# Second norm's low half by TensorE and ScalarE, logits from stacked weights, routing without its sum, and a new instruction order, in a one-core adaLN + SSM + MoE block

## The chip, the core and the metric

One core of one Trainium2 chip runs the whole kernel. The metric is the device time of one execution in microseconds. Below, PE is TensorE (PEld its weight loads), DVE is VectorE, ACT is ScalarE, POOL is GpSimd and SP is the engine that issues most DMAs.

## The reference

The input `x` is 8 sequences of 1024 rows of 256 channels. Everything is float32. Cut to what matters here:

```python
h = layernorm(x) * (1 + ca) + sa                  # ca, sa, ga, cb, sb, gb: per sequence, from c
x = x + ga * ssm(h)                               # scan over the rows, 16 states per channel:
                                                  #   state = exp(dt*A)*state + dt*u*B;  y = sum_n state*C
h = layernorm(x) * (1 + cb) + sb                  # the second norm
probs = softmax(h @ Wg)                           # 8 experts
top_vals, top_idx = top_k(probs, 2)
gates = top_vals / sum(top_vals)
x = x + gb * sum_over_the_two(gates * (h @ We[e] + be[e]))
```

## The kernel before

**Stages.** The rows are cut into 16 stages of 512 rows, two for each sequence. A stage is worked on channel-major: two halves `j` of 128 channels on the partitions, 512 rows along the free dimension. Stage `s` has three parts, and the parts of neighbouring stages overlap:

- `front(s)`: the first norm, its transposes into channels (`trans1`), modulation on ACT, the projection `proj` (L915), its copy `xd` (L920), the spill of B and C to DRAM and the broadcast loads `load B, C` (L1002, tile `bc`, a ring of 5 buffers), `dt` by softplus on ACT (L952) and `du` on POOL (L958).
- `state(s, n)` for n = 0 to 15: `v = du * B` on POOL (L1012, ring of 4), two `a = exp(dt*A)` on ACT (L1023, ring of 3), two scans on DVE (L1034), and the product with C, either on DVE (L1044, tile `hcD`, two instructions) or on POOL (L1049, tile `hs`, one instruction). `C_ENG` says which: in the middle 6 of 16 states go to POOL in a sequence's first stage and 7 in its second, in the last two stages 4. A `bc` buffer comes free when the product with C is done. PE adds the 16 products up in PSUM (L1097, tile `y`).
- `back(s)`: `x + y` on DVE, statistics, the second norm, its transposes (`trans2`, L852, tile `pt` in PSUM), the split of `h` into a rounded high part and a low part (below), the logits, the routing (L1225 to L1244, sixteen small steps, of which fifteen on DVE, and `gates` on DVE), and 16 expert pairs of six matmuls each (L1310: high x high, high x low weight, low x high weight). For all but the last stage ACT scales each pair by its gate (L1388, `wt`), PE adds the transposed results up (L1398, `ma`), ACT multiplies by gb (L1405), PE turns them back (L1413, `pf`) and a POOL DMA adds them to the output in DRAM. In the last stage, which is done in two parts of 256 rows, DVE adds the pairs up instead (L1333).

**The split.** PE runs these matmuls in a rounded float32 (fp32r). `hi` is ACT's modulation of `pt` written as fp32r; ACT then modulates `pt` again in place, exactly; DVE subtracts (L1169): `lo = pt - hi`. The PSUM tiles `pt`, `pe`, `pl`, `pf` and others share a ring of two banks, `psm`.

**The order.** Each instruction is recorded with a planned cost and a due time from the table `DUE`; a planner (`Plan.emit`) plays the engines through, always takes the ready instruction with the earliest due time, and so fixes one order for each engine, which is what the program holds. On the chip each engine works through its own list in order and waits where an operand or a buffer isn't ready.

Of the kernel before, what the change touches and what calls it, by code (L numbers as in the profile page):

```python
# [30 lines left out]
AHEAD = 1010.84  # L31
PATIENCE = {"ACT": 0.15, "DVE": 0.31, "PE": 0.32, "POOL": 0.26, "SP": 0}
# [5 lines left out]
    "-1/2": -610.4,  # L38
    "load c": -1959.77,
    "load wmod0": -1959.2,  # L40
    "load wmod1": -1903.73,
    "load wmod2": -1904.33,
    "load wmod3": -1902,
    "load W_x": -1905.67,
    "load W_dt": -1902.95,
    "load b_dt": -1896.67,
    "load A": -1896.69,
    "load D": -1905.33,
    "load Wg": 23.65,
    "Wg hi": 25.6,  # L50
    "Wg lo": -1879.07,
    "c^T": 19.14,
    "exp c": 576.64,
    "1 + exp c": -171.26,
    "1 / c": -583.34,
    "silu c": 49.75,
    "mod1": 597.1,
    "mod1 out": 214.25,
    "mod1 + 1": -23.47,
    "mod2": -1859.82,  # L60
    "mod2 out": -158.07,
    "mod3": 229.79,
    "mod3 out": -128.45,
    "mod3 + 1": -812.43,
    "ga0": -205.9,
    "ga1": -118.55,
    "ga2": -138.57,
    "ga3": -194.1,
    "gb0": 46.87,
    "gb1": 211.85,  # L70
    "gb2": -132.77,
    "gb3": -2055.94,
    "ga mod": -1469.96,
    "ga mod D": 75.2,
    "1 / ga": -434.12,
    "gb^T": -1935.95,
    "gb out": -1918.95,
    "gb store": -2004.44,
    "W_x^T": 597.29,
    "W_x out": -3.67,  # L80
    "W_dt^T": -1851.32,
    "W_dt out": -85.73,
    "exp A": -10.89,
    "-A": -388.67,
    "be rows": -3.96,
    "be hi": -24.41,
    "be lo": -124.92,
    "be": 74.87,
    "eps": -5318.24,
    "gates hi": (-1934.68, -2774.13, 20.33, -39.94, 880.55),  # L90
    "gates lo": (-26.36, -2354.31, -688.15, -51.05, -108.76),
    "load be": -1860.49,
    "iw": -610.42,
    "load x": (-1905.45, -1873.57, -1877.87, -1851.67, -345.66),
    "stats1": (224.71, 130.11, 139.36, -25.7, -59.05),
    "aggr1": (213.04, 114.8, -308.72, -24.67, 2.36),
    "before1": (-102.85, 91.85, 2.54, -14.87, -18.75),
    "rstd1": (-1104.41, -1916.02, -121.49, -268.12, -120.91),
    "shift1": (-507.66, -410.48, -1091.47, 527.46, 48.83),
    "norm1": (-144.62, -217.6, 35.93, 471.97, 36.59),  # L100
    "trans1_0": (-1936.2, -1160.43, -2075.71, -328.08, -365),
    "modg_0": (-1701.88, 396.46, -461.17, -6.71, -105.52),
    "modD_0": (-1695.18, -131.34, -462.04, -397.38, -105.23),
    "trans1_1": (-388.21, -18.09, -54.78, -626.82, -11.83),
    "modg_1": (-50.33, -1935.21, -197.83, -9.86, -10.79),
    "modD_1": (-11.21, -1916.99, -81.27, -9.63, -23.55),
    "W_x / ga": (66.75, 401.9, 25.85, -49.61, 434.89),
    "proj": (-596.85, -706.64, -714.41, -84.24, -74.21),
    "rows": (-2173.39, -2045.69, -3586.53, -10.82, -2052.7),
    "spill": (-4069.73, -5330.21, -46.16, -311.17, 432.09),  # L110
    "dt0": (-45.16, -658.43, -1891.19, -1934.24, -76.75),
    "softplus0": (-1126.61, -39.94, -137.57, -2844.14, -16.53),
    "dt1": (-2318.21, -2801.94, -207.93, -1934.26, -398.3),
    "softplus1": (-1126.2, -132.53, -379.84, -2844.16, -28.04),
    "du": (-195.14, -2811.82, -615.21, -365.67, -2224.29),
    "load B, C": (-5316.63, -1003.95, -1855.19, -4111.06, -3714.47),
    "v": (-12.17, -164.66, 175.11, 576.96, 952.78),
    "a0": (-22.27, -4.61, -6.54, -5.76, -3.99),
    "a1": (-22.41, -4.9, -6.15, -6.69, -4.35),
    "scan0": (-141.18, -335.17, -38.46, -51.65, -37.62),  # L120
    "keep0": (-1141.13, -1001.73, -2670.6, -1274.64, -1043.43),
    "C0": (-158.99, -48.75, -78.37, -397.8, -49.3),
    "scan1": (254.21, -7.15, -37.67, -52.31, -38.52),
    "keep1": (-281.8, -71.4, -191.93, -1247.6, -175.93),
    "C1": (-927.57, -102.36, -383.08, -272.81, -85.21),
    "C": (-434.46, -982.76, -611.91, -346.76, -4070.99),
    "y D": (-45.12, -33.67, -1893.89, -3.99, 105.31),
    "y": (-692.43, -142.1, -4.58, -4.37, -52.76),
    "y C": (-691.09, -2044.02, -79.98, -1517.96, -52.81),
    "load We": -1855,  # L130
    "We hi": -9.52,
    "We lo": -13.87,
    "x + y": (-1479.33, -1886.74, -1168.73, -231.3, 149.03),
    "store x": (-922.68, -81.4, -352.75, -1815.49, -3867.78),
    "stats2": (-1494.52, -143.82, -1171.26, -54.3, -45.3),
    "aggr2": (-211.14, -109.77, -383.59, -45.32, -9.65),
    "before2": (-6.93, 939.25, -95.98, -81.58, 4.88),
    "rstd2": (-1311.51, -927.35, -919.37, -30.48, -1009.27),
    "shift2": (-289.83, -684.01, -16.58, -27.32, -1671.91),
    "norm2": (-1.27, -217.09, 3.69, -457.58, 32.8),  # L140
    "trans2_0": (-119.41, -234.62, -25.53, -50.95, -76.58),
    "hi0": (-141.55, -203.81, -1226.77, -71.08, -264.52),
    "mod2_0": (-2325.4, 23.63, -1516.83, 17.71, 8.96),
    "lo0": (-954.37, -2006.41, -590.6, 934.22, -43.41),
    "trans2_1": (-68.72, -46.84, -1.98, -2278.83, -10.41),
    "hi1": (1.23, -85.95, -1275.97, -1245.79, 101.74),
    "mod2_1": (-321.5, -1489.76, -82.34, 2.7, -325.68),
    "lo1": (-1141.17, -296.15, -3856.65, 5.32, -1526.54),
    "logits^T": (-724.23, -896.69, -969.16, -194.29, -2895.23),
    "logits out": (-1885.54, -25.88, 4.38, -1907.25, -252.75),  # L150
    "logits": (-1228.11, -85.65, -1913.27, -106.24, -61.81),
    "route": (-1101.97, -1134.93, -1307.99, -656.85, -170.03),
    "gates": (-23.84, -155.06, -1508.55, -606.87, -165.13),
    "gates^T": (407.78, -236.26, -474.82, -43.28, -53.64),
    "gates out": (-77.16, -201.21, -201.01, -1117.77, 23.17),
    "biases": (-1847.78, -40.94, -21.25, 21.25, 22.67),
    "expert0": (-47.23, -150.46, 2.39, -24.85, 59.33),
    "weigh0": (-1667.95, -187.39, -1697.15, 581.79, -169.94),
    "sum0": (154.3, 300.84, -65.34, 25.8, 428.26),
    "gb": (-58.36, -0.34, -1235.11, 1080.88, -11.47),  # L160
    "turn": (45.89, -1931.1, -368.57, -9.4, 45.02),
    "out": (15.32, -128.7, -182.23, -5.57, 44.86),
    "expert1": (-18.1, -22.7, 0.47, 22.62, 93.37),
    "weigh1": (-2663.68, -186.81, -1239.07, -35.96, -23.31),
    "sum1": (49.93, -21.05, 3.3, -9.9, -95.83),
    "store": (96.93, -341.18, 142.45, -243.69, -21.12),
    "load gb": (-157.01, -157.01, -157.01, -157.01, -165.58),
    "last bias": -13.22,
    "last": 89.02,
    "last expert": -11.99,  # L170
    "last store": -219.81,
# [246 lines left out]
def kernel(  # L418
# [62 lines left out]
    wg_hi = cp.tile([P, DC, E], F32R, name="wg_hi")  # L481
    wg_lo = cp.tile([P, DC, E], F32R, name="wg_lo")
# [6 lines left out]
    eps = cp.tile([P, 1], F32, name="eps")  # L489
    gb_d = dram.tile([B, D], F32, name="gb_d", bufs=1)  # L490
# [18 lines left out]
    def setup():  # L509
# [20 lines left out]
        add("eps", "DVE", 0.01, lambda: nc.vector.memset(eps, EPS), w=[("eps",)])  # L530

# [35 lines left out]
        def wg():  # L567
# [6 lines left out]
        wgf = [w.rearrange("p k e -> p (k e)") for w in (wg_hi, wg_lo)]  # L574
        add("Wg hi", "ACT", 0.2, lambda: nc.scalar.copy(wgf[0], wg()), r=[wg_k], w=[("wg", 0)])
        add(
            "Wg lo", "DVE", 0.08,
            lambda: nc.vector.tensor_tensor(wgf[1], wg(), wgf[0].bitcast(F32), ALU.subtract),
# [267 lines left out]
    def to_channels(i, s, j, t, part):  # L846
        xn, pt, tg = ("xn", i, s, part), ("pt", i, s, part, j), part[1] - part[0]

        def f():
            p = psum(pt)  # L850
            for k in range(tg):
                nc.tensor.transpose(  # L852
                    p[:, k * P : (k + 1) * P], T[xn][:, k, j * P : (j + 1) * P], ident
                )

        plan.add(
            f"trans{i}_{j}", "PE", 0.11 * tg, t, f, r=[xn + (k,) for k in range(tg)], w=[pt],
            ring=[("psm", pt)] + [(k, (k, s, part)) for k in (("g", "gd") if i == 1 else ("hi", "lo"))],
        )
# [264 lines left out]
    def back(s, t, part):  # L1124
# [37 lines left out]
        def mod_hi(j):  # L1162
            modulate(new("hi", hi, [P, DC, CL], F32R)[:, j], 2, s, j, modT[:, 3:], part)
# [37 lines left out]
        def logits_out():  # L1201
            nc.scalar.copy(new("lg", lgt, [E, CL])[:, :cl], T[pl][:E, :cl])
# [322 lines left out]
```

## Time and profile before

| what | us |
|---|---|
| median of 3 runs (1077.4 to 1081.53) | 1079.51 |
| the profiled execution, by its run time | 1078.12 |
| its span, first to last instruction | 1076.2 |
| DVE busy in the span | 976.5 |
| PE busy | 948.7 |
| POOL busy | 928.3 |
| ACT busy | 840.0 |
| first scan starts (end of the lead-in) | 32.9 |
| stages 1 and 2 (from the first scan of one stage to that of the next) | 67.4 and 65.8 |
| stages 3 to 12 together | 611.4 |
| stages 13 to 15, to the end of the scans | 193.5 |
| from there to the end (the tail) | 46.8 |

"Busy" is the time in which an engine runs an instruction. The stages are cut at the first scan of each stage on DVE; each holds the back part of the stage before it. The average of stages 3 to 12 is 61.1 us.

### The profile page before, as it was taken

How to read it: one execution, taken by the hardware profiler on the slowest of the kernel's cores; microseconds unless marked ns; L12 is line 12 of the kernel's file. 1: busy time of each engine (PE TensorE's matmuls, PEld its weight loads, DVE VectorE, ACT ScalarE, POOL GpSimd, SP SyncE). 2: the span in 40 equal slices, each digit the busy share in tenths (PEclk: the TensorE clock that was granted, in tenths of full speed). 3: DMA queues.
4: the chain of work that ended last, by engine and by line, in shares of the span. 5: the costliest groups of instructions: out<-in, count | busy, mean ns of one | idle time of the engine just before them, and what ended most of it. 6: DMA issues, size and time to landing. Idle time of an engine off the chain costs nothing. (4 is left out here: it accounts for less than half of the span.)

```text
span 1076.2 us, 16579 instructions
## 1 busy us (share of the span) xinstructions
PE 948.7 (88%) x5525; PEld 746.9 (69%) x5525; DVE 976.5 (91%) x1506; ACT 840.0 (78%) x1835; POOL 928.3 (86%) x454
## 2 busy tenths in 40 slices
PE   6556897997989989898999999898998989899997
PEld 3444675775777858686776868677786767777765
DVE  4699897989999999999999999999999998989957
ACT  5755577887799877988799887988898788887651
POOL 3899776899999999899999999999999989888700
PEclk9666798998999989999999999999899999999999
DMA  6445333447545555454554653554555554365202
GB/s 208 143 176 176 137 139 112 144 165 192 173 162 160 176 159 177 131 185 157 153 202 120 208 164 138 169 179 157 151 195 143 175 155 159 119 178 153 102 1 44
DMA packets 67956, 165.13 MB, mean 153 GB/s; under 512 B 7056, under 2 KB 34080, under 8 KB 67872
## 3 DMA queue, kind: packets, MB, share of 16 engines
q1 hardware_dynamic: 59952, 156.23, 43.1%
q0 software_dynamic: 7920, 7.87, 5.3%
q8 instruction: 43, 0.70, 0.3%
q14 instruction: 41, 0.34, 0.1%
HBM read 146.76 MB, written 17.31 MB: 152 GB/s over the span
## 5 line engine op out<-in xcount | busy, mean ns | idle before, releaser
L1012 POOL TENSOR_TENSOR v<-du,bc 128x1024 f32<-128x1024 f32 x255 | 610.2, 2423 | 54.5 <-DMA bc<-bcd 35.7
L1023 ACT ACTIVATE a<-dt,negA 128x512 f32<-128x512 f32 x512 | 347.1, 692 | 54.8 <-DVE hcD L1044 45.0
L1049 POOL TENSOR_TENSOR hs<-hs,bc 128x1024 f32<-128x1024 f32 x96 | 232.3, 2419 | 16.2 <-ACT carry L1040 5.0
L1044 DVE TENSOR_TENSOR hcD<-a,bc 128x512 f32<-128x512 f32 x320 | 213.6, 682 | 15.1 <-ACT carry L1040 7.4
L1388 ACT ACTIVATE wt<-pe,G 128x256 f32<-128x256 f32 x480 | 200.8, 468 | 33.8 <-PE pe L1310 26.5
L1034 DVE TENSOR_TENSOR_SCAN a<-a,v 128x512 f32<-128x512 f32 x166 | 195.7, 1212 | 23.5 <-ACT a L1023 17.7
L1097 PE MATMUL y<-ident,hcD 128*128 128x128 f32 x1280 | 185.8, 286 | 30.9 <-DVE hcD L1044 30.7
L1034 DVE TENSOR_TENSOR_SCAN a<-a,carry,v 128x512 f32<-128x512 f32 x154 | 196.3, 1278 | 9.8 <-ACT a L1023 7.0
L1097 PEld LDWEIGHTS y<-ident,hcD 128*128 128x128 f32 x1280 | 154.8, 148 | 49.0 <-DVE hcD L1044 37.8
L1310 PE MATMUL pe<-we_hi,hi 128*128 128x512 f32 x512 | 181.7, 436 | 3.4 <-DVE lo L1169 1.1
L1310 PE MATMUL pe<-we_hi,lo 128*128 128x512 f32 x512 | 162.6, 399 | 0.0
L1310 PE MATMUL pe<-we_lo,hi 128*128 128x512 f32 x512 | 162.1, 398 | 0.0
L1398 PE MATMUL ma<-ident,wt 128*128 128x128 f32 x960 | 139.7, 274 | 0.6 <-ACT wt L1388 0.4
L1097 PE MATMUL y<-ident,hs 128*128 128x128 f32 x768 | 111.0, 290 | 24.0 <-POOL hs L1049 23.4
L1097 PEld LDWEIGHTS y<-ident,hs 128*128 128x128 f32 x768 | 92.0, 148 | 50.9 <-POOL hs L1049 40.5
L1398 PEld LDWEIGHTS ma<-ident,wt 128*128 128x128 f32 x960 | 112.5, 140 | 21.4 <-issue 4.6
L1034 DVE TENSOR_TENSOR_SCAN hs<-a,carry,v 128x512 f32<-128x512 f32 x102 | 126.0, 1268 | 1.3 <-ACT a L1023 1.3
L1310 PEld LDWEIGHTS pe<-we_lo,hi 128*128 128x128 f32 x512 | 97.1, 190 | 23.7
L1310 PEld LDWEIGHTS pe<-we_hi,lo 128*128 128x128 f32 x512 | 96.9, 189 | 23.7
L1034 DVE TENSOR_TENSOR_SCAN hs<-a,v 128x512 f32<-128x512 f32 x90 | 106.4, 1206 | 4.3 <-ACT a L1023 4.2
L1310 PEld LDWEIGHTS pe<-we_hi,hi 128*128 128x128 f32 x512 | 82.0, 192 | 16.6 <-ACT wt L1388 4.1
L822 ACT ACTIVATE xn<-x,ln 128x256 f32<-128x256 f32 x128 | 72.9, 598 | 1.6 <-POOL ln L814 1.6
(126 smaller groups left out, 969.2 us busy)
## 6 DMA issues: line engine op xcount, KB each, us to landing
bc<-bcd SPq DMA_DIRECT2D x256, 512.0 KB, 4.0
x<-in_L_attn_u_dram SPq DMA_DIRECT2D x16, 512.0 KB, 4.0
out_dram<-x SPq DMA_DIRECT2D x15, 512.0 KB, 3.0
out_dram<-of POOLq DMA_DIRECT2D x15, 512.0 KB, 9.1
wf<-in_L_ffn_We_dram SPq DMA_DIRECT2D x8, 256.0 KB, 4.0
wm<-in_L_wmod_dram SPq DMA_DIRECT2D x2, 512.0 KB
bcd<-xd SPq DMA_DIRECT2D x32, 32.0 KB, 3.7
wm<-in_L_wmod_dram SPq DMA_DIRECT2D x2, 256.0 KB, 6.0
```

The source lines that it names most:

```text
L822: nc.scalar.activation(new("xn", xn, [P, TG, D])[:, k, :], T[x][:, k0 + k, :], AF.Identity, bias=T[ln][:, 1, o + k : o + k + 1], scale=T[l ...
L1012: nc.gpsimd.tensor_tensor(new("v", v, [P, DC, CL])[:, :, :cl], T["du", s][:, :, :cl], both(T[bc][:, 0, :cl]), ALU.mult,)
L1023: nc.scalar.activation(new("a", a + (j,), [P, CL])[:, :cl], T["dt", s][:, j, :cl], AF.Exp, scale=negA[:, j, n : n + 1],)
L1034: nc.vector.tensor_tensor_scan(part(j), T[a + (j,)][:, :cl], T[v][:, j, :cl], init, ALU.mult, ALU.add)
L1044: nc.vector.tensor_tensor(new("hcD", hc, [P, DC, CL])[:, j, :cl], part(j), T[bc][:, 1, :cl], ALU.mult)
L1049: nc.gpsimd.tensor_tensor(o, o, both(T[bc][:, 1, :cl]), ALU.mult)
L1097: nc.tensor.matmul(new("y", y, [P, 2, D])[:, k % 2, j * P : (j + 1) * P], T[src][:, j, k * P : (k + 1) * P], ident, is_transpose=True, sta ...
L1310: nc.tensor.matmul(pe, T[v][:, j, k * P : (k + 1) * P], w[:, j, 2 * q : 2 * q + 2, :].rearrange("p e d -> p (e d)"), start=n == 0, stop=n ...
L1388: nc.scalar.activation(new("wt", wt, [P, 2, D])[:, i, :], T["pe", s, part, q, k][:, i * D : (i + 1) * D], AF.Copy, scale=T[G][:, k, e : e ...
L1398: nc.tensor.matmul(o[:, j, (k % 2) * P : (k % 2 + 1) * P], T["wt", s, q, k][:, i, j * P : (j + 1) * P], ident, is_transpose=True, start=Fa ...
```

## The change

- **Low part.** ACT first modulates `pt` in place, then copies it to `hi` in fp32r. A PE matmul with a constant minus identity (`less`) adds `-hi` to the PSUM bank that still holds `pt`, and ACT copies the difference out as `lo`. The DVE subtraction is gone. The transposes of `trans2` are written so that the accumulation stays open.
- **Logits.** The two parts of `Wg` lie side by side, 16 columns. `hi` is multiplied by all 16, `lo` by the first 8: four matmuls of 512 columns in place of six. The small transposes behind them become matmuls with a constant `fold` that adds the two halves.
- **Routing.** The sum of the two chosen weights is 1 + the second one, since the largest is exp(0). An ACT instruction, early in the routing, computes it; the reduction on DVE (L1239) is gone.
- **Order.** All due times, the look-ahead `AHEAD` and `PATIENCE` are new. In the planner an expert pair of stage `s` comes after the last expert of stage `s-1` of the half before it (`ex`) and after the turn-back of an earlier half (`td`).
- `C_ENG`, the rings and all else are as they were.

```diff
-AHEAD = 1010.84
-PATIENCE = {"ACT": 0.15, "DVE": 0.31, "PE": 0.32, "POOL": 0.26, "SP": 0}
+AHEAD = 1196.62
+PATIENCE = {"ACT": 0.15, "DVE": 0.4, "PE": 0.29, "POOL": 0.23, "SP": 0}
...
+        add("-I", "ACT", 0.25, lambda: nc.scalar.activation(negI, ident, AF.Copy, scale=-1.0), w=[("negI",)])
...
+        add("fold", "DVE", 0.07, lambda: nc.vector.reduce_sum(fold, ident[: 2 * E, : 2 * E].rearrange("p (i e) -> p e i", i=2), AX.X), w=[("wg", 2)])
...
                 nc.tensor.matmul(
+                    p[:, k * P : (k + 1) * P], T[xn][:, k, j * P : (j + 1) * P], ident,
+                    is_transpose=True, start=k == 0, stop=i == 1 and k == tg - 1, skip_group_check=True,
...
         def mod_hi(j):
-            modulate(new("hi", hi, [P, DC, CL], F32R)[:, j], 2, s, j, modT[:, 3:], part)
+            nc.scalar.copy(new("hi", hi, [P, DC, CL], F32R)[:, j, :cl], T["pt", 2, s, part, j][:, :cl])
...
+        def less(j):
+            nc.tensor.matmul(
+                T["pt", 2, s, part, j][:, :cl], negI, T[hi][:, j, :cl], start=False, stop=True,
+                skip_group_check=True,
+            )
         def low(j):
-            nc.vector.tensor_tensor(
-                new("lo", lo, [P, DC, CL], F32R)[:, j, :cl], T["pt", 2, s, part, j][:, :cl],
-                T[hi][:, j, :cl].bitcast(F32), ALU.subtract,
-            )
+            nc.scalar.copy(new("lo", lo, [P, DC, CL], F32R)[:, j, :cl], T["pt", 2, s, part, j][:, :cl])
...
-            for v, w in products:
+            for v, m in ((hi, 2 * E), (lo, E)):
                 for j in range(DC):
                     nc.tensor.matmul(
-                        lg[:E, :cl], (wg_hi, wg_lo)[w][:, j, :], T[v][:, j, :cl],
-                        start=n == 0, stop=n == 3 * DC - 1,
+                        lg[:m, :cl], wg_2[:, j, :m], T[v][:, j, :cl], start=n == 0, stop=n == 2 * DC - 1,
+                        skip_group_check=True,
...
-                nc.tensor.transpose(
-                    T[pl][:, k * E : (k + 1) * E], T[lgt][:, k * P : (k + 1) * P], ident[:E, :E]
+                nc.tensor.matmul(
+                    T[pl][:, k * E : (k + 1) * E], T[lgt][:, k * P : (k + 1) * P], fold, start=True, stop=True
...
-            lambda: red(col(3), view(1), AX.X, ALU.add),
-            lambda: nc.vector.reciprocal(col(3), col(3)),
+            nc.scalar.activation(col(3), col(1), AF.Identity, bias=1.0)
...
+            turns = [("ex", s - 1)] if s else []
+            if 2 * s + p > 2:
+                turns.append(("td", s - 2 + p, 1 - p))
...
-                        r=[hi, lo] + wes, w=[pe], ring=("psm", pe), duty=0.88, cold=1.76,
+                        r=[hi, lo] + wes + turns,
+                        w=[pe] + ([("ex", s)] if m == ends else []), ring=("psm", pe), duty=0.88, cold=1.76,
```

What the new due times make of the order, by reading both programs' instruction lists: expert pairs that stand before the last product with C of stages 1, 2 and 3 on PE are 13, 28 and 41 before and 9, 25 and 41 after, and from there on both have 16 for each stage until the end, where 237 of 240 become 236. The projection of stage 3 stands on PE behind 24 pairs before and behind 18 after; that of later stages, up to stage 13, behind the same number of pairs but behind 10 to 11 of the 16 sums of the stage in place of 8 to 10.

## The prediction

> **What bounds the kernel now.** I read the page's first part, then the time cut by stages, then the waits of the two busiest engines over the middle stages, then single shapes.
>
> ```profile
> PE 948.7 (88%) x5525; PEld 746.9 (69%) x5525; DVE 976.5 (91%) x1506; ACT 840.0 (78%) x1835; POOL 928.3 (86%) x454
> ```
>
> DVE looks like the bound, but 91% is an average over parts with different limits. Cut by stages (columns: stretch, length, then busy time and instructions of PE, PEld, DVE, ACT, POOL, then granted PE clock, DMA share, GB/s):
>
> ```profile
> 0.00:32.90 32.90, 23.05 (x82) 16.48 (x82) 10.89 (x58) 20.62 (x40) 16.27 (x21) 0.88 0.74 231
> 32.90:91.30 58.40, 30.86 (x127) 23.25 (x127) 54.28 (x61) 33.55 (x78) 52.97 (x25) 0.68 0.39 139
> 91.30:158.70 67.40, 56.65 (x289) 44.18 (x289) 61.37 (x90) 44.12 (x82) 53.49 (x26) 0.81 0.42 147
> 158.70:224.50 65.80, 57.15 (x337) 44.45 (x335) 57.03 (x89) 52.89 (x129) 53.65 (x27) 0.92 0.42 148
> 224.50:835.90 611.40, 563.34 (x3404) 446.46 (x3403) 584.48 (x870) 520.66 (x1138) 585.80 (x277) 0.98 0.53 165
> 835.90:1029.40 193.50, 179.11 (x1110) 144.22 (x1109) 179.45 (x255) 153.44 (x331) 162.52 (x77) 1.00 0.46 142
> 1029.40:1076.20 46.80, 38.49 (x186) 27.89 (x184) 28.97 (x86) 14.73 (x41) 3.57 (x7) 0.97 0.13 26
> ```
>
> In the ten middle stages DVE (584.5) and POOL (585.8 of 611.4, 96%) are equally full, and the change takes nothing from POOL. That is the main point: whatever DVE loses, POOL still needs 585.8. What it waits for there, and what DVE waits for:
>
> ```profile
> POOL v L1012 <- DMA bc<-bcd: 8.5, 9, 1.8
> POOL v L1012 <- DVE pl L1233: 2.8, 1, 2.8
> DVE a L1034 <- ACT a L1023: 4.4, 4, 1.7
> DVE a L1034 <- POOL v L1012: 3.5, 4, 1.2
> ```
>
> POOL's longest wait is for the B, C loads. A load can start only when the product with C of the state five earlier has freed its buffer. POOL's timeline shows the cycle:
>
> ```profile
> 499.59 2.35 POOL L1049 TENSOR_TENSOR hs<-hs,bc 128x1024 f32<-128x1024 f32 x1
> 501.91 2.35 POOL L1012 TENSOR_TENSOR v<-du,bc 128x1024 f32<-128x1024 f32 x1
> 504.48 0.25 POOL L1270 TENSOR_TENSOR gs<-G,gs 128x32 fp32r<-128x32 f32 x1 [0.22 <-ACT gs L1267]
> 506.10 4.70 POOL L1012 TENSOR_TENSOR v<-du,bc 128x1024 f32<-128x1024 f32 x2 [1.36 <-DMA bc<-bcd]
> ```
>
> The product ends at 501.9, and the `v` that needs the buffer starts at 506.1: about 4.1 us for release, load and landing. With only one `v` in between, POOL stands still for 1.4 to 1.8 us.
>
> **The change part by part.** The rows that price it:
>
> ```profile
> L1169 DVE TENSOR_TENSOR lo<-pt,hi 128x512 fp32r<-128x512 f32 x30 | 20.4, 680 | 1.4 <-ACT pt L863 1.2
> L1419 ACT COPY of<-pf 128x512 f32<-128x512 f32 x30 | 17.5, 584 | 6.1 <-PE pf L1413 6.0
> L863 ACT ACTIVATE hi<-pt,modT 128x512 fp32r<-128x512 f32 x30 | 23.3, 782 | 2.0 <-PE pt L852 2.0
> L1195 PE MATMUL pl<-hi,wg_lo 128*8 128x512 f32 x30 | 9.6, 404 | 0.0
> ```
>
> *DVE.* Gone are 30 x 0.680 + 4 x 0.422 (the last stage's 256 columns) = 22.1 us of L1169, and 17 reductions of 0.19 = 3.2. Per middle stage that is 2 x 0.680 + 0.19 = 1.55, 15.5 in the ten: DVE falls to 569, 93%.
>
> *ACT.* Two copies for `lo` are added, two modulations become copies, one small instruction (0.184, as L1227) comes in the routing. With the nearest copy out of PSUM, 0.584: 2 x 0.584 - 2 x (0.782 - 0.584) + 0.184 = +0.95 a stage. ACT is idle (611.4 - 520.7) / 10 = 9.1 a stage, so the load is free. Its waits are not (second rival). The Trainium skill speaks against this move: "ScalarE: Activation LUTs", section Rules for kernel authors, gives additions to VectorE and budgets about 0.3 us and 0.83 ns an element for ScalarE, by my estimate 0.725 for 512. The trace shows a copy at 0.584 against DVE's subtraction at 0.680. By the page ACT would gain 4 x 0.14 = 0.6 more a stage, still inside its idle time, and the sum would stay.
>
> *PE.* `less` is two matmuls of 512 columns a stage, 0.40 each by L1195's row; the logits lose two at 0.40. Nil. No row shows a matmul with 16 output columns; 8 and 128 both take 0.40, so I take no difference. The `fold` matmuls replace transposes one for one (0.21 each); between nothing and, at the 0.30 that other small transposes take, 0.4 us a stage, hidden in PE's (611.4 - 563.3) / 10 = 4.8 of idle time. Without that cover: +6 in all.
>
> *Lead-in (to 32.9).* Setup steps move on all queues, SP's loads too. The first scan now stands behind five small DVE steps of the second modulation. They cost some 4.5 us before, but stood between the first scans then. What is late next is the second scan, at 39.3 before; POOL's first `v` follows a softplus that is put behind four normalisations (2.1 us). I take 0, with -2 and +2 as bounds.
>
> *Stages 1 and 2* are 133.2 long where two middle stages take 122.3: 10.9 too many. Stage 2 is short of data for stage 3: PE worked 28 expert pairs in the first two stages, and the projection of stage 3 stood behind 24 of them; POOL then waited for the loads (13.2 us in the two stages, up to 5.4 at once). Now it is 25 pairs, and the projection stands behind 18, five states earlier. The three pairs fall into stage 3, where PE is idle for 7 us. The bounds are all 10.9 and nothing; I take half, -5.5. A rule speaks against it: "TensorE: Matmul & The Clock Gate", section Part 1, says that the array's clock stays halved until a window of about 3.4 us has been busy. The rows agree: 0.68 in stage 0, 0.81 in stage 1, 1.0 later. With 9 pairs in place of 13 in stage 1, PE is less busy and may stay slow. By that rule I would put 0 in place of -5.5.
>
> *Stages 3 to 12.* POOL is idle for 25.6. The part that the buffers force: in the order of before, a product and the `v` that reuses its buffer have one `v` between them in six places, and some 3.8 us in three; with 4.1 needed, that makes 10.8. In the new order it is nine places and five: 16.1. So the stages can't go below 585.8 + 16.1 = 601.9, a gain of at most 9.5; if the other 14.8 of waiting (on late scans, behind blocks of routing) stay whole, they lose 5.3. DVE's 1.55 a stage should remove part: I take half of the 14.8, and get -2.1.
>
> *Stages 13 to 15.* POOL has 31 us to spare, DVE and PE are level at 179 of 193.5. DVE loses 6 x 0.680 + 3 x 0.19 = 4.7, PE one expert pair (some 1.5). I take -3; bounds -4.7 and, for a 3.9 us stop of POOL that the new order makes in stage 14 (a product and its `v` with almost nothing between), +3.
>
> *Tail.* Behind the last sum PE now has 20 pairs to do instead of 19, but three fewer `ma` groups. The chain of the first part (transpose, modulate, `hi`, `less`, `lo`, logits) gets two hops between ACT and PE where DVE stood ready: +1.5. For the second part an expert pair (1.7 us) stands between `hi` and `less`, and PE then has seven pairs behind the second turn of the gates instead of six. I take +3, bounds 0 and +6.
>
> Sum: 0 - 5.5 - 2.1 - 3 + 3 = -7.6. The profiled execution took 1078.1 (its span 1076.2), so 1070.5; the median, 1.4 above it, would give 1071.9. I say 1071.
>
> **The rivals.**
>
> *No change (POOL keeps the time).* POOL is as full as DVE, the new order forces 5.3 more waiting, stages 1 and 2 lose by the slow clock what they gain in order, the tail takes 3: -2 to +5, 1077 to 1084. For it: the 96% row. Against it: POOL was not the limit in stages 1, 2 and 13 to 15.
>
> *Slower: `lo` waits on ACT for `less`.* In most middle stages an expert pair (six matmuls, 1.7 us) stands on PE right before one of the two `less`, and only 0.9 to 2.3 us of ACT work stands between `hi` and `lo`. ACT works in order: behind a late `lo` stand the `a` of the next scans, with a ring of three, and DVE waits for them. 30 halves at up to 1.5 us. It decides from 0.43 us for each half that reaches the scans: 13 us, which turns -7.6 into +5.4. At 0.75 the time is 1071 + 22 = 1093. Against it: DVE waits for `a` only 6.6 us in the ten stages now, and the planner put work there.
>
> *Larger gain (DVE was the pace).* All of DVE's 25.3 comes out, since POOL's waits were DVE's lateness: 1078 - 25 + 3 = 1056. Against it: the floor of 601.9.
>
> **How the numbers follow.** Forecast 0.54, with its own range of 1060 to 1074; larger gain 0.08; no change 0.20; slower 0.18. About 0.5% (5.4 us) is what a measurement of this kernel can tell from no change; faster means under 1074.1, slower over 1084.9. The range goes from 1056 to 1087: it leaves out half of the larger gain and two thirds of the slower case, some 0.17 together.
>
> **What would show it.** Right: DVE busy near 951, POOL still near 928, stages 1 and 2 near 127 together, the ten middle stages between 602 and 612 with POOL over 96% busy, the tail near 50. Wrong: long waits of DVE for L1036's `a`, of ACT's `lo` for PE, or a first scan after 35.

## The result, and the profile after

The changed kernel took 1088.83 us (median of four runs, 1086.65 to 1090.82), beside 1078.76 for before in the same runs: a ratio of 1.0075, 95% interval 1.0053 to 1.0098. It is slower, by 10 us in the medians and 8 by the ratio, where 1071 was forecast with a range to 1087. Its profiled execution took 1090.8 (span 1089.0), 12.8 more in span than the profiled one of before.

First the busy times of the page (engine, busy us, share of the span, instructions):

```profile
PE 965.8 (89%) x5589; PEld 766.8 (70%) x5589; DVE 952.4 (87%) x1456; ACT 855.6 (79%) x1887; POOL 927.7 (85%) x454
```

The work moved as worked out: DVE lost 24.1 us (22.1 + 3.2 forecast), ACT gained 15.6 (0.95 for each stage is 15.2), POOL kept its 928. Only PE is off: nil was said, with at most some 6 for `fold`; it gained 17.1. So the time was not lost to work on DVE, ACT or POOL. The stages show where it went (stretch, length, then busy us and instructions of PE, PEld, DVE, ACT, POOL, granted PE clock, DMA share, GB/s); the last cut is the end of the last scan, which lies at 1027.9 in before. The cut used there ahead of the prediction, 1029.4, is 1.5 us later; by the cut of this table its 193.5 and 46.8 become 192.0 and 48.3, and its last row becomes the one that stands below these, by itself:

```profile
0.00:32.40 32.40, 19.99 (x86) 14.31 (x86) 13.94 (x64) 20.07 (x40) 14.60 (x20) 0.96 0.73 224
32.40:86.50 54.10, 29.82 (x122) 22.26 (x123) 50.89 (x56) 34.03 (x79) 53.88 (x25) 0.66 0.45 157
86.50:152.50 66.00, 52.06 (x296) 41.32 (x296) 63.02 (x97) 44.81 (x84) 54.35 (x26) 0.91 0.45 150
152.50:212.60 60.10, 54.86 (x311) 43.45 (x310) 53.01 (x76) 52.36 (x128) 54.03 (x26) 0.89 0.45 151
212.60:838.50 625.90, 579.82 (x3467) 464.14 (x3465) 569.68 (x842) 532.42 (x1177) 585.13 (x277) 0.97 0.54 163
838.50:967.20 128.70, 121.65 (x723) 96.63 (x722) 114.32 (x164) 107.97 (x239) 118.39 (x56) 0.96 0.49 150
967.20:1032.70 65.50, 61.68 (x396) 51.15 (x395) 59.44 (x81) 46.44 (x97) 43.78 (x22) 1.00 0.40 121
1032.70:1089.00 56.30, 45.95 (x201) 33.48 (x199) 28.12 (x82) 17.45 (x50) 3.57 (x7) 0.90 0.11 21
```

```profile
1027.90:1076.20 48.30, 39.44 (x192) 28.64 (x191) 29.69 (x87) 15.16 (x42) 3.57 (x7) 0.97 0.12 25
```

| stretch | before | after | difference | forecast |
|---|---|---|---|---|
| lead-in | 32.9 | 32.4 | -0.5 | 0 |
| stage 0 | 58.4 | 54.1 | -4.3 | not in the sum |
| stages 1 and 2 | 133.2 | 126.1 | -7.1 | -5.5 |
| stages 3 to 12 | 611.4 | 625.9 | +14.5 | -2.1 (-9.5 to +5.3) |
| stages 13 to 15, to the last scan's end | 192.0 | 194.2 | +2.2 | -3 (-4.7 to +3) |
| tail | 48.3 | 56.3 | +8.0 | +3 (0 to +6) |

At the start of stage 3 the new kernel is 11.9 us ahead. It then loses 14.5 in the ten middle stages, where POOL's work is the same to 0.7 us and DVE has 14.8 less. Both stand still instead: DVE for 56.2 us (26.9 in before), POOL for 40.8 (25.6). What POOL and DVE wait for there (in all, times, longest):

```profile
POOL v L1025 <- DMA bc<-bcd: 19.6, 15, 3.5
POOL gs L1293 <- ACT gs L1290: 6.0, 4, 2.4
```

```profile
DVE a L1047 <- ACT a L1036: 16.4, 18, 1.9
DVE hcD L1057 <- ACT carry L1053: 11.0, 26, 1.4
DVE a L1047 <- POOL v L1025: 8.3, 10, 2.4
DVE hs L1047 <- ACT a L1036: 3.2, 7, 0.7
```

and, of before, the two rows of DVE that the prediction does not show:

```profile
DVE hcD L1044 <- ACT carry L1040: 2.2, 6, 0.7
DVE hs L1034 <- ACT a L1023: 2.2, 3, 1.4
```

POOL's wait for the loads has gone from 8.5 to 19.6. One of them in the timeline of POOL:

```profile
798.86 2.37 POOL L1062 TENSOR_TENSOR hs<-hs,bc 128x1024 f32<-128x1024 f32 x1
801.19 2.40 POOL L1025 TENSOR_TENSOR v<-du,bc 128x1024 f32<-128x1024 f32 x1
807.08 2.35 POOL L1025 TENSOR_TENSOR v<-du,bc 128x1024 f32<-128x1024 f32 x1 [3.50 <-DMA bc<-bcd]
```

The product with C ends at 801.2, one `v` follows, and the next `v` has to wait for the load into the buffer that the product freed. That takes 5.9 us here, where the prediction put 4.1.

Some of these waits are put down to another releaser, so I added them up another way: for each `v` whose buffer a product on POOL had held, the idle time right before it, if there was any. In the middle stages of before that is 12 times, 14.1 us in all, with 3.9 to 5.2 us from the product's end to the start of `v`; in after 16 times, 25.2 us, mostly 3.8 to 5.9, once 9.7 (there the load was issued late). In the others the load is issued within 0.03 us of the product's end, so the rest is the load itself. One of the waits that the profile puts down to PE:

```profile
568.82 2.38 POOL L1062 TENSOR_TENSOR hs<-hs,bc 128x1024 f32<-128x1024 f32 x1
...
571.99 2.90 POOL L1025 TENSOR_TENSOR v<-du,bc 128x1024 f32<-128x1024 f32 x1
576.62 2.35 POOL L1025 TENSOR_TENSOR v<-du,bc 128x1024 f32<-128x1024 f32 x1 [1.74 <-PE pv L959]
```

Here 5.4 us pass from the product's end (571.2) to the `v`.

### The profile page after: what moved, and what is told of

It is laid out like the page before. It is cut to its first block, busy times and chain, and to the rows that moved or that the text cites. A ratio compares the mean times of both kernels' runs of the same rounds, so it can differ in the third digit from the quotient of the medians.

```text
span 1089.0 us, 16751 instructions
## 1 busy us (share of the span) xinstructions
PE 965.8 (89%) x5589; PEld 766.8 (70%) x5589; DVE 952.4 (87%) x1456; ACT 855.6 (79%) x1887; POOL 927.7 (85%) x454
## 5 line engine op out<-in xcount | busy, mean ns | idle before, releaser
L1062 POOL TENSOR_TENSOR hs<-hs,bc 128x1024 f32<-128x1024 f32 x96 | 228.6, 2382 | 13.1 <-DVE hs L1047 6.3
L1047 DVE TENSOR_TENSOR_SCAN a<-a,v 128x512 f32<-128x512 f32 x166 | 197.3, 1217 | 26.4 <-ACT a L1036 14.1
L1333 PE MATMUL pe<-we_hi,hi 128*128 128x512 f32 x512 | 184.7, 442 | 2.7 <-ACT dt L965 1.4
L1421 PE MATMUL ma<-ident,wt 128*128 128x128 f32 x960 | 142.9, 275 | 0.8 <-ACT wt L1411 0.8
L1110 PE MATMUL y<-ident,hs 128*128 128x128 f32 x768 | 112.9, 294 | 31.2 <-POOL hs L1062 30.6
```

The lines of the kernel that those rows point to most:

```text
L1047: nc.vector.tensor_tensor_scan(part(j), T[a + (j,)][:, :cl], T[v][:, j, :cl], init, ALU.mult, ALU.add)
L1062: nc.gpsimd.tensor_tensor(o, o, both(T[bc][:, 1, :cl]), ALU.mult)
L1110: nc.tensor.matmul(new("y", y, [P, 2, D])[:, k % 2, j * P : (j + 1) * P], T[src][:, j, k * P : (k + 1) * P], ident, is_transpose=True, sta ...
L1333: nc.tensor.matmul(pe, T[v][:, j, k * P : (k + 1) * P], w[:, j, 2 * q : 2 * q + 2, :].rearrange("p e d -> p (e d)"), start=n == 0, stop=n ...
L1421: nc.tensor.matmul(o[:, j, (k % 2) * P : (k % 2 + 1) * P], T["wt", s, q, k][:, i, j * P : (j + 1) * P], ident, is_transpose=True, start=Fa ...
```

## Experiments

In all of them the planner is not run; its order is written out as a list, so that parts and order can be exchanged one by one:

```diff
-        while len(order) < len(ops):
...
-            best, soon = None, dma.next()
...
+        order = ORDER
```

"Parts" are the three changes of the code (low part, logits, routing), "order" is the sequence in which all queues get their instructions. "Spliced" is the order of after up to the first scan of stage 4, and the order of before from there:

```diff
-ORDER = before
+first = after[: after.index(("scan0", stage 4, state 0))]
+ORDER = first + [step for step in before if step not in first]
```

Where a part is taken alone, its hunks of the change are applied and the others are not; a step that only one version has stands beside the step that it follows (`less` behind its `hi`). The ratio is to before, in the same runs, with its 95% interval. Before itself took 1078.5 to 1081.1 in these groups of runs, so the ratios are what to compare.

| parts | order | buffers for B, C | us | ratio |
|---|---|---|---|---|
| before | before | 5 | 1078.8 | 1 |
| after | before | 5 | 1091.0 | 1.0120 (1.0100 to 1.0140) |
| before | after | 5 | 1093.4 | 1.0136 (1.0116 to 1.0156) |
| after | after | 5 | 1088.8 | 1.0075 (1.0053 to 1.0098) |
| before | spliced | 5 | 1070.7 | 0.9927 (0.9899 to 0.9956) |
| after | spliced | 5 | 1078.5 | 0.9998 (0.9975 to 1.0022) |
| low part alone | spliced | 5 | 1082.2 | 1.0014 (0.9991 to 1.0036) |
| logits alone | spliced | 5 | 1074.8 | 0.9955 (0.9927 to 0.9983) |
| routing alone | spliced | 5 | 1071.0 | 0.9916 (0.9888 to 0.9943) |
| before | before | 6 | 1071.2 | 0.9925 (0.9909 to 0.9941) |
| before | after | 6 | 1082.6 | 1.0036 (1.0010 to 1.0061) |
| after | after | 6 | 1070.6 | 0.9908 (0.9884 to 0.9932) |
| before | spliced | 6 | 1062.4 | 0.9844 (0.9824 to 0.9863) |
| low part alone | spliced | 6 | 1074.2 | 0.9943 (0.9924 to 0.9962) |
| after | spliced | 6 | 1070.3 | 0.9919 (0.9892 to 0.9946) |
| after | after, last stage as before | 6 | 1070.9 | 0.9921 (0.9890 to 0.9951) |

**Order or parts.** The first pair exchanges them.

> All parts of before (the low part by the subtraction on DVE, six logit matmuls, four transposes, the sum of the gates) on each queue in the order of after; a step that both have stands where after has it. Theory ORDER: the loss of after (middle ten stages 611.4 to 625.9, tail 48.3 to 56.3) is made by the new order of the queues, so it stays: 1085 to 1095, middle at least 620, tail 54 to 57. Theory PARTS: the loss is made by the new steps themselves (the low part waits for PE on ACT, PE has 17 us more work), and the order only brings the 11.9 us that stages 0 to 2 gained: 1066 to 1072, middle near 611.

> All parts of after in the order of before; the matmul with minus identity stands right behind its copy of the high part. ORDER: 1073 to 1081 (DVE has 25 us less and most of that hides behind POOL), middle 605 to 613, tail 48 to 51. PARTS: 1090 to 1100, since the middle loses its 14.5 us and the gain of stages 0 to 2, which is the order's, is missing; middle 622 or more, with DVE waiting for the decay factors of ACT.

Measured: 1093.4 and 1091.0. The old parts in the new order lose as ORDER said (middle 623.0, tail 54.6). But the new parts in the old order lose too, as PARTS said, though at other places: middle 615.5 (+4.1), stages 13 and 14 +3.3, lead-in +2.6 (before with six buffers, below, has +1.7 there with no other change, so part of this may be the execution), tail 50.0 (+1.7). Either one alone costs 1.2 to 1.4%, both together 0.75%: the two don't add. With the old parts the new order loses about as much in the middle and tail as after does, and it is the only order in which the new parts gain something (0.6%). That the sizes are alike doesn't make the cause the same; the sixth buffer, below, parts them.

**The start alone.**

> Parts of before; the order of after up to the first scan of stage 4 (273.2 us in after, 286.2 in before), the order of before from there. Both theories: 1078.8 - 13.0 = 1066, if the start of after is worth what its trace shows and is not given back behind the joint; 1072 or more if some of it is.

> Parts of after, the same splice. ORDER: 1060 to 1068, as the old parts in this splice or a little less. PARTS: 1066 + 14 = 1080.

Measured: 1070.7 and 1078.5. The start of the new order is worth 0.7% with nothing else changed, about 8 us; part of the expected 13 is given back behind the joint (stage 4 takes 65.0, 60.3 in before). The new parts cost 0.7% in this order; their trace has 1.1 us of that in the middle stages, 4.1 in stage 14 and 2.7 behind it.

**Which part.**

> The spliced order, with one of the three new parts: the low part by PE and ACT. With the old parts this order took 1070.7, with all three new ones 1078.5. Theory LOW (the 7.8 us belong to the low part: two more hops between ACT and PE, and the copies stand before the next decay factors on ACT): 1076 to 1079. Rival FOLD (they belong to the logits, whose last step takes 17.4 us of PE where it took 7.0): 1070 to 1072 here. Rival SPREAD (each part a third): 1073.

> The spliced order, with only the stacked logits. LOW: 1070 to 1072 (two matmuls of 0.40 go, and the eight small ones take 0.65 us a stage more: level). FOLD: 1075 to 1078. SPREAD: 1073.

> The spliced order, with only the routing without its sum: 3.2 us less on DVE, 3.0 more on ACT. LOW and FOLD: 1068 to 1071. SPREAD: 1073.

Measured: 1.0014, 0.9955 and 0.9916, beside 0.9927 with none. The low part costs 0.9%, all that the three cost together. The routing without its sum can't be told from nothing; the logits neither, since the intervals overlap, though a third of the cost (0.3%) can't be ruled out for them. LOW stands; FOLD and SPREAD don't, since each needs the low part alone to cost little or a third.

**The ring of the loads.** One more buffer takes away what makes POOL wait, and nothing else:

```diff
-    "dt": 2, "du": 2, "bc": 5, "v": 4, "hs": 3, "carry": 2, "hcD": 3,
+    "dt": 2, "du": 2, "bc": 6, "v": 4, "hs": 3, "carry": 2, "hcD": 3,
```

> After itself, with six buffers for the B, C loads in place of five, every queue in the same order. Theory RING: the middle stages of after are long because POOL waits for loads that wait for a product with C (19.6 us of waits in the ten stages, 8.5 before): those waits go, the middle falls from 625.9 to 612 or less, the time to 1074 or less. Rival A (DVE waits for ACT's decay factors, 19.6 us against 6.6, whatever POOL does): POOL's waits go to other releasers, and the time falls by less than 5, to 1084 or more.

Measured: 1070.55, ratio 0.9908: 18 us less. The ten middle stages of this run (611.4 in before), and what is left of POOL's wait for loads in them:

```profile
210.98:821.04 610.06, 572.50 (x3459) 461.87 (x3458) 568.35 (x842) 530.99 (x1173) 586.00 (x277) 0.97 0.55 167
```

```profile
POOL v L1210 <- DMA bc<-bcd: 0.9, 1, 0.9
```

and DVE's waits for ACT:

```profile
DVE a L1232 <- ACT a L1221: 11.3, 15, 1.8
DVE hcD L1242 <- ACT carry L1238: 6.3, 22, 0.4
...
DVE hs L1232 <- ACT a L1221: 3.1, 6, 0.7
```

The middle falls from 625.9 to 610.1 with every queue in the same order and the same work, and POOL's wait for loads from 19.6 to 0.9. RING is right for after, rival A is not: DVE's waits for ACT (`a` and carry together) fall along with POOL's, from 30.6 to 20.7 us.

> Before itself (its parts, its order) with six buffers for the B, C loads. In its ten middle stages the first drive that finds its buffer held by a product with C waits 12 times, 14.1 us in all (16 times, 25.2 us, in after). If those waits are time: 1078.8 - 14 = 1065, or 1068 if DVE (584.5 of 611.4) gives some of it back. Rival (DVE is as full as POOL, so its work keeps the time): 1074 to 1079.

> Before's parts in after's order, now with six buffers; with five it took 1.0136 of before. If the ring is what the new order loses by: 1078.8 x 1.0136 - 18 = 1075 or less, as much gained as after gained (1.0075 to 0.9908). If DVE, with 22 us of work more than in after, is late by itself: above 1082.

> Before's parts, after's order up to stage 4, before's order from there, six buffers. Gains of the splice (0.9927 of before) and of the ring (10 to 14 us) together: 1058 to 1062. If both gains are the same waits: 1066 to 1070.

Measured: 0.9925, 1.0036 and 0.9844. Before gains 8 us from the sixth buffer where after gains 18. With it, before and after are level (0.9925 and 0.9908). The old parts in the new order gain 11, less than after; they end at the 1082 that was named for a late DVE. In the new order, then, the new parts are worth 1.3% with six buffers; that this is the lighter DVE is argued, not shown by itself.

The traces say where the ring counts. In the middle stages the waits for a buffer held by POOL fall from 14.1 to 1.0 us in before, from 25.2 to 0.9 in after and from 21.8 to 1.6 with the old parts in the new order. But the stages get shorter by only 2.9 us (611.4 to 608.5), 15.8 and 3.2 (623.0 to 619.8). A counted wait is time only where nothing else would have made POOL wait. With the old parts in the new order something else does: DVE's waits for ACT's `a` and carry stay at 20.5 us with either ring, and POOL's `hs` waits 10.7 us for ACT's carry where it waited 1.3. So it is the new order together with the new parts that the ring held; what keeps the old parts long in that order stays open.

The old parts in the spliced order with six buffers are the fastest kernel of this study, 1062.4; the two gains add.

**How the low part costs.** Two runs repeat the spliced pair where the ring no longer holds POOL:

> Spliced order, old parts but for the low part by PE and ACT, six buffers. With five the low part cost 0.9927 to 1.0014, 9.4 us. If it costs by itself (DVE stands for decay factors that ACT computes behind the copies): 0.9844 to about 0.993, 1071. If it costs through the ring (later scans, later products, later loads): 0.9844 to 0.987, at most 1066.

> Spliced order, all new parts, six buffers. Low part by itself: 0.992, about 1070. Through the ring: at most 0.987, 1065.

Measured: 0.9943 and 0.9919, beside 0.9844 with the old parts. The cost stays at 1.0%, so it isn't the ring's. In the middle stages of the low part alone DVE has 9.5 us less work (573.6 for 583.1) and they are 8.0 longer (617.7 for 609.7); stages 14 and 15 and the tail add 4 more. What DVE waits for in the middle, old low part:

```profile
DVE a L1221 <- ACT a L1210: 5.2, 5, 1.7
DVE hcD L1231 <- ACT carry L1227: 4.6, 6, 2.7
```

and new low part:

```profile
DVE hcD L1237 <- ACT carry L1233: 11.6, 15, 2.9
DVE a L1227 <- ACT a L1216: 9.8, 14, 1.7
```

Between the starts of one state's scans and the next's, the new low part adds 0.9 us in state 7 of the even middle stages (6.87 for 5.96), 4.5 of the 8.0 us in the five of them, and at most 0.24 in their other states. In the odd ones state 7 loses 0.9 too, but states 5 and 6 win 0.7 back. In state 7 the second half is split. At the passage from state 6 to state 7, with the old low part (spliced, five buffers, stage 6) DVE does

```profile
426.99 2.32 DVE L1217 TENSOR_TENSOR_SCAN a<-a,v 128x512 f32<-128x512 f32 x2
429.21 1.27 DVE L1227 TENSOR_TENSOR hcD<-a,bc 128x512 f32<-128x512 f32 x2
430.40 0.68 DVE L1352 TENSOR_TENSOR lo<-pt,hi 128x512 fp32r<-128x512 f32 x1
431.00 2.33 DVE L1217 TENSOR_TENSOR_SCAN a<-a,v 128x512 f32<-128x512 f32 x2
433.24 0.67 DVE L1227 TENSOR_TENSOR hcD<-a,bc 128x512 f32<-128x512 f32 x1
```

and with the new one (same place and order):

```profile
425.67 2.61 DVE L1227 TENSOR_TENSOR_SCAN a<-a,v 128x512 f32<-128x512 f32 x2 [0.41 <-ACT a L1216]
428.19 1.27 DVE L1237 TENSOR_TENSOR hcD<-a,bc 128x512 f32<-128x512 f32 x2
429.73 2.35 DVE L1227 TENSOR_TENSOR_SCAN a<-a,v 128x512 f32<-128x512 f32 x2 [0.28 <-ACT a L1216]
432.57 0.69 DVE L1237 TENSOR_TENSOR hcD<-a,bc 128x512 f32<-128x512 f32 x1 [0.49 <-ACT carry L1233]
```

From the first scan to the last product (start to start) it is 6.25 before and 6.90 after, though 0.68 of work is gone. ACT's queue tells why. With the old low part:

```profile
429.40 0.76 ACT L1046 ACTIVATE pt<-pt,modT 128x512 f32<-128x512 f32 x1
430.07 1.30 ACT L1206 ACTIVATE a<-dt,negA 128x512 f32<-128x512 f32 x2
...
432.62 0.18 ACT L1223 COPY carry<-a 128x1 f32<-128x1 f32 x1
```

With the new one:

```profile
427.32 0.78 ACT L1056 ACTIVATE pt<-pt,modT 128x512 f32<-128x512 f32 x1
...
428.39 0.64 ACT L1356 CAST hi<-pt 128x512 fp32r<-128x512 f32 x1
428.87 0.76 ACT L1216 ACTIVATE a<-dt,negA 128x512 f32<-128x512 f32 x1
429.63 0.58 ACT L1368 CAST lo<-pt 128x512 fp32r<-128x512 f32 x1
430.11 0.70 ACT L1216 ACTIVATE a<-dt,negA 128x512 f32<-128x512 f32 x1
...
432.37 0.17 ACT L1233 COPY carry<-a 128x1 f32<-128x1 f32 x1
```

The `lo` copy now stands between the two `a` of the next state. From the first of them to the carry that the last product waits for, ACT needs 3.5 us where it needed 2.55, as much more as state 7 is longer. DVE's subtraction had partly filled time in which DVE had to wait anyway: in the old version the products ended at 430.5, the first `a` at 430.8. Without it DVE stands, and ACT, which is the one that is late here, has more to do. This is read from the traces; no run moves the copy to another place.

**The tail.**

> After with six buffers and its own order up to the last state of stage 14, then the order of before. The last stage and the tail took 64.2 + 53.7 us in after with six buffers, and 63.7 + 50.0 where the new parts ran in before's order: 4.2 us less, 0.987 of before, 1064 to 1067. If the tail's length is made by the new parts: 1070, no change.

Measured: 1070.9, no change that can be told (0.9921 beside 0.9908). The trace has the 4.2 us that were expected at the end (stage 15 and tail 63.7 + 50.0, not 64.2 + 53.7), but a stage 14 of 68.9 in place of 66.7 ahead of them, and no run here says whether the splice makes that.

## Why the prediction was wrong

**Stages 3 to 12, the step that failed.** -2.1 was said, +14.5 came. The mechanism was named (the product, the release, the load, with 4.1 us needed, and more places of that kind in the new order), but the term was mis-sized, in two ways. POOL's idle time was to be 16.1 us of forced waiting and 7.4 of other; it was 25.2 and 15.6.

First, the forced waiting was worked out from a fixed 4.1 us: 10.8 in the old order, 16.1 in the new one, 5.3 more (with a `v` of 2.35 the same working gives 11.4 and 17.3). Measured are 14.1 and 25.2, 11.1 more. The places were the right ones. The nine with one `v` in between waited 16.4 us. But the five with some 3.8 us in between, put at 0.3 each, waited 7.3 in all, because loads there took 4.8 to 5.4 us (the example at 576.62 is one of them); two further places add 1.5. The 4.1 was one load; others took up to 5.9 us from product to `v`, and a schedule that stands on the shortest case waits at each longer one. Second, half of the other 14.8 us of POOL's waiting was to go since DVE is lighter. By the measured count the other waiting was 11.5 before, and it rose to 15.6. DVE's saved 14.8 us turned whole into standing still: its waits for `v` rose from 3.5 to 8.3 us, those for ACT's `a` and carry from 8.8 to 30.6. The sixth buffer shows that the ring was what made the time: with it the middle is 610.1, near the 609.3 that the prediction expected of it with five.

The signs that were named fit this: DVE (952.4) and POOL (927.7) busy as said, stages 1 and 2 as said; the ten middle stages and the tail not, and the long waits of DVE for `a`, named as a sign of being wrong, are there (19.6 us, 6.6 in before).

**The rivals.** The one that ended slower had the right sign, but not the mechanism as it was put: `lo` was to wait on ACT for `less` at 0.43 us or more for each half. In the middle stages of after `lo` waits 2.9 us in all, six times. What the low part does cost, where it costs, comes from ACT's order: the `a` behind its copies, not the copy behind PE. And in the new order this is not what made after slow: with a sixth buffer and the same low part the middle is 610.1.

**The forecast's start.** The gain in stages 1 and 2 was right (-7.1 for -5.5, "near 127" together: 126.1). The run of the old parts in the new order puts most of it on the order: 128.4 there, 133.2 in before and with the new parts in the old order. The size was half of the bounds, a choice, so that it came so near is luck. The clock did not decide it. It was granted 0.91 in stage 1 of after, 0.81 in before; but with the old parts in the new order it was 0.82, and stage 1 took 66.0 us as in after. So what the prediction drew from the Trainium skill ("TensorE: Matmul & The Clock Gate", section Part 1), 0 in place of -5.5, did not come, neither at 0.91 nor at 0.82. (The rows of before read 0.92 in stage 2 and 0.98 in the middle, not 1.0.) Stage 0 wasn't in the sum and gave 4.3: POOL, idle for 5.4 us there before, is idle for 0.2. This gain is not in every execution: of the thirteen traces whose start has the new order, eleven have a stage 0 of 52.7 to 54.3 us, and two one of 58.9, in which POOL stands for 5.1 us before `du`.

**The tail.** +3 was said, +8.0 came. The runs split it: new parts in the old order 50.0 (+1.7); the new order with six buffers, whose clock stays whole, 53.7 (+3.7 more); after itself 56.3. The last 2.6 come with a clock at half speed (granted 0.50) for 10.2 us, from 1064.2 on, behind a stretch in which PE was busy for 1.96 of 3.7 us. The old parts in the new order have 54.6 with 3.4 us of half clock and, with six buffers, 55.3 with 6.8, so the length follows the clock there as well; by these numbers the new parts add little to the tail in this order. The stretch and most of the slow one:

```profile
1060.70:1064.40 3.70, 1.96 (x12) 1.15 (x11) 3.38 (x8) 1.90 (x5) 0.00 (x0) 0.97 0.01 2
1064.40:1073.60 9.20, 8.00 (x22) 5.44 (x22) 2.87 (x16) 1.86 (x7) 1.55 (x2) 0.50 0.51 86
```

The second part's chain begins 28.0 us behind the last scan (24.3 in before), with all eight expert pairs of the first part done ahead of it, so that one pair of its own (at 1066.4) is all that covers its routing:

```profile
1060.74 0.41 PE L864 MATMUL pt<-ident,xn 128*128 128x128 f32 x2
1062.24 0.39 PE L1182 MATMUL pt<-hi,negI 128*128 128x256 f32 x1 [1.08 <-ACT hi L1176]
1063.09 0.66 PE L1436 MATMUL pf<-ident,mo 128*128 128x128 f32 x4 [0.46 <-ACT lo L1188]
```

**PE's work.** The matmuls with `fold` were bounded at 0.4 us a stage. They are 17.4 us in all where the transposes were 7.0, 0.65 a stage; each is two instructions (128 for 64 blocks). `less` takes 14.7 (0.453 for 512 columns, not 0.40), where the logits save 10.8. That makes 14.3 of the 17.1 us; the rest is spread over rows that both programs have:

```profile
L1224 PE MATMUL pl<-fold,lg 16*128 16x8 f32 x128 | 17.4, 257 | 0.0
L1182 PE MATMUL pt<-hi,negI 128*128 128x512 f32 x30 | 13.4, 453 | 0.7 <-ACT carry L1053 0.6
L1188 ACT CAST lo<-pt 128x512 fp32r<-128x512 f32 x30 | 17.7, 592 | 3.5 <-PE pt L1182 3.4
```

The logits taken alone are level for PE (10.4 more, 10.8 less) and couldn't be told from nothing; whether PE's idle time hides `less`, no run shows. The copy out of PSUM took 0.592, near the 0.584 of the row of before; the 0.725 worked out from the Trainium skill ("ScalarE: Activation LUTs", section Rules for kernel authors) was too high. That row is for an ACTIVATE with its bias as an operand, which a copy has not; the modulations in place, which have one, took 0.75 in the median.

## What to carry to other kernels

Where an engine's work is cyclic through a ring of buffers, price the time from the release to the next use by its spread, not by one load, and count the places in the new order that have no slack: a sixth buffer was worth 8 us to before and 18 to after. Don't take counted waits for time, either: in the middle stages nearly all of them went with that buffer, and 2.9 us of 14.1 came out in before, 15.8 of 25.2 in after. Taking work off an engine gained nothing here at a place where that work filled a wait, and cost where the engine that took it over was the one being waited for; look for what stands next on the receiver's queue. And where a change brings its own order, exchange order and parts before blaming either: here each alone cost over 1%, and the useful pieces were the start of the new order and one more buffer.

## What was not expected of the hardware

- An ordinary f32 matmul of a block of 16 rows into 8 columns is recorded as two instructions and cost PE 0.136 us of busy time each (17.4 / 128), a transpose of a block of 8 rows one and 0.109 (7.0 / 64).
- The clock fell to 0.50 for 10.2 us behind 3.7 us in which PE was 53% busy and its longest idle time was 1.08 us. The busy share alone does not decide it: in the tail of after with six buffers PE was 55% busy for 3.4 us (1047.2 to 1050.6), and the clock stayed whole.
- The load of B and C took 4.0 us from issue to landing in the median in before, 4.3 in after, and 4.7 and 4.5 in the two with six buffers (the landing is known for a third of the loads); the same product-to-`v` loop took 3.8 to 5.9 us within one run.
